# A sparse graph-attention kernel on one core: q copied a block ahead, list places read a step later, smaller last chunks, and the last block's values in one go

## The chip, the core and the metric

The kernel runs on one core of one Trainium2 chip. The time is the device time in microseconds (us) from the first to the last instruction; lower is better. The engines are named as in the profile: PE multiplies matrices, DVE does elementwise work and reductions, ACT does copies and nonlinear functions, POOL issues the indexed transfers (gathers), SP issues plain ones. Each engine works through its own list of instructions in the order in which the program emits them and waits on semaphores for the others.

## The reference, cut to what matters

The input is a table x of 3327 rows by 256 and an adjacency matrix of 3327 by 3327 in which about 0.5% of the entries are one. Layer 0 is a simple attention with one score per row; layers 1 to 3 are graph transformer layers of one form with weights of their own:

```python
# layers 1, 2, 3 (8 heads of 32)
qkv = layer_norm(x, g1, be1) @ w_qkv
q, k, v = ...
scores = einsum('nhd,mhd->hnm', q, k) * SCALE
scores = where(adj != 0, scores, -inf)
attn = softmax(scores, axis=-1)
out = einsum('hnm,mhd->nhd', attn, v).reshape(n, 256)
x = x + out @ w_proj + b_proj
h2 = layer_norm(x, g2, be2)
x = x + gelu(h2 @ w1 + b1) @ w2 + b2          # w1: 256 x 1024
```

## The kernel before

The kernel does not form the 3327 by 3327 scores. A first stage (layer 0 included) reads the adjacency matrix, makes for each row the list of its neighbours (up to 40), and sorts the rows by the length of their lists: `place` below is where a row's rank in that sort is read from counts that PE has summed up in PSUM. The sorted rows stand in 26 blocks of 128; a block needs as many slots as its longest list has entries, from 40 down to 10, 448 slots in all. Block 0, with 40 slots, comes last in the order of work.

In each of layers 1 to 3 the k and v rows of the neighbours are fetched slot by slot with indexed gathers on POOL (448 a layer), four slots to a tile, ten tiles in a ring (121 tiles a layer). A tile's way:

```python
def scores(self, b, s0):                     # one tile: k.q on DVE
    ...
    nc.vector.tensor_mul(k, k, self.q[b]...)                 # line 1320
    nc.vector.tensor_reduce(self.sc[b][:, s0:s0 + n, :], ...)  # line 1321
def softmax(self, b):                        # after a block's last tile
    nc.vector.tensor_tensor_reduce(sc, sc, pad[b]..., mx)    # line 1332
    nc.scalar.activation(sc, sc, AF.Exp, bias=mx, scale=-1.0)  # line 1335
def take_q(self, b):                         # q of a block into PSUM, two buffers
    nc.scalar.copy(self.q[b], t2[:, b, D:2 * D])             # line 1306
def weights(self, b):  ...                   # 1/sum on DVE, lines 1341 to 1348
def values(self, b, s0):                     # one tile: weighted v, summed on PE
    nc.vector.tensor_mul(vw, v, self.wp[b]...)               # line 1361, vw has 3 buffers
    for s in range(0, n, 2):
        nc.tensor.matmul(self.po[b], ident, vw[...])         # line 1366
    self.issue()                             # the tile is free: gathers of a later one
    if s0 + GS >= S:
        self.short += self.block(b)          # projection of the block, 9 short steps
```

`block(b)` queues nine short steps (copy, fold, transpose, copy, project on PE at line 1402, and at the end the add into x on DVE at line 1406). When the last block of a *chunk* has been added, the chunk's long steps are queued: layer norm, transposes, the two feed-forward products with gelu (lines 1445, 1451, 1468; PE works on all rows of the chunk at once), the add (line 1486), and, if a layer follows, its layer norm and q, k, v products (line 1498), after which k and v go to memory. `some()` is called once per tile and spreads these steps over the tiles of the blocks that follow; `rate` is how much of them is taken per tile:

```python
for n in [CB - 1] + [CB] * ((NB - CB - 2) // CB) + [2, 1]:   # 3, 4,4,4,4,4, 2, 1 blocks
    ...
# in add(), at the end of a chunk:
at = ORDER.index(b) + 1
turns = sum(len(slots[i]) for i in ORDER[at:at + CB])
turns = 5 if at == NB - 1 else turns - 2
self.rate = sum(cost for cost, _ in self.long) / max(turns, 1)

def some(self):
    if self.short: self.short.pop(0)()
    self.credit = min(self.credit + self.rate, 8.0)
    while self.long and self.credit > 0:
        cost, step = self.long.pop(0); self.credit -= cost; step()
    if self.short: self.short.pop(0)()

def run(self):
    ...
    for k, b in enumerate(ORDER):
        for g in slots[b]:
            self.scores(*g)
            if g == slots[b][-1]:
                self.softmax(b)
                if k + 1 < NB: self.take_q(ORDER[k + 1])
            for i in wait: wait[i] += 1
            for _ in range(2 if len(todo) > NBUF // 2 or b == 0 else 1):
                if todo and wait[todo[0][0]] > 1: value()
            self.some()
        todo += slots[b]; wait[b] = 0
    while todo:                              # the ten tiles of block 0
        value()
        self.some()
    self.rate = 4.0
    while self.short or self.long: self.some()
```

A layer's gathers read the k and v of all rows, so the next layer's first gather comes after the last chunk of the layer before.

Of the kernel before, what the change touches and what calls it, by code (L numbers as in the profile page):

```python
# [8 lines left out]
FP = mybir.dt.float32  # L9
# [3 lines left out]
ALU = mybir.AluOpType  # L13
AX = mybir.AxisListType
# [3 lines left out]
P = 128  # L18
# [14 lines left out]
NB = (N + P - 1) // P  # L33
# [25 lines left out]
NBUF = 10  # L59

CB = 4
# [462 lines left out]
def sparse_path(ctx, tc, ins, out, dram, flag):  # L524
    nc = tc.nc
# [13 lines left out]
    rank = const.tile([P, NB], FP, name="rank")  # L539
# [83 lines left out]
    with tc.tile_pool(name="a", bufs=1) as a, tc.tile_pool(name="aw", bufs=2) as aw, \  # L623
# [56 lines left out]
        nd = LMAX + 1  # L680
# [3 lines left out]
        OH = a.tile([P, NB, nd], BF, name="OH")  # L684
        rest_tri = a.tile([P, P], BF, name="rest_tri")
# [155 lines left out]
        class Group:  # L841
# [36 lines left out]
            def soft(self):  # L878


                g, n, b0 = self.g, self.n, self.blocks[0]

                def sv(name):
                    t = aw.tile([P, 4], FP, tag="s_" + name, bufs=1, name=f"s_{name}_{g}")
                    return t[:, :n]

                sg = S.s[:, b0:b0 + n]
                dg = deg[:, b0:b0 + n]
                nc.vector.tensor_copy(dg, self.acc[:, :n, H0])
                top = sv("top")  # L890
                nc.vector.tensor_scalar(top, dg, float(LMAX), None, ALU.min)
                nc.vector.tensor_tensor(OH[:, b0:b0 + n, :],
                                        num[:, None, :nd].to_broadcast([P, n, nd]),
                                        top[:, :, None].to_broadcast([P, n, nd]), ALU.is_equal)

                at = places[:, :4 * nd].rearrange("p (b k) -> p b k", k=nd)
                for j in range(n):
                    i = b0 + j
                    add = [(tri, i)] + [(ones_bf, k) for k in range(b0, i)]
                    if g:  # L900
                        add += [(rest_tri, i - 4)] + [(ones_bf, k) for k in range(i - 3, b0)]
                    for lhsT, m in add:
                        nc.tensor.matmul(at[:, j, :], lhsT, OH[:, m, :], start=False, stop=True,
                                         skip_group_check=True)
                t = aw.tile([P, 4, nd], FP, tag="place", bufs=1, name=f"place_{g}")[:, :n]
                nc.vector.tensor_mul(t, at[:, :n, :], OH[:, b0:b0 + n, :])
                nc.vector.tensor_reduce(rank[:, b0:b0 + n], t, AX.X, ALU.add)
                if b0 + n == NB:
                    nc.tensor.matmul(at[:, n - 1, :], rest_tri, OH[:, NB - 1, :], start=False,
                                     stop=True, skip_group_check=True)  # L910
                    S.all = at[:, n - 1, :]
                non, ga, fa, m1, m0, tt, mx = (
                    sv(k) for k in ("non", "ga", "fa", "m1", "m0", "tt", "mx"))
                nc.vector.tensor_scalar(non, dg, -1.0, float(N), ALU.mult, ALU.add)
                nc.vector.tensor_scalar(ga, dg, 0.0, None, ALU.is_gt)
                nc.vector.tensor_scalar(fa, non, 0.0, None, ALU.is_gt)
                nc.vector.tensor_scalar(tt, ga, -NEG0, NEG0, ALU.mult, ALU.add)
                nc.vector.tensor_mul(m1, sg, ga)
                nc.vector.tensor_add(m1, m1, tt)
                nc.vector.tensor_scalar(tt, fa, -1.0, 1.0, ALU.mult, ALU.add)  # L920
                nc.vector.tensor_mul(m0, sg, tt)
                nc.vector.scalar_tensor_tensor(m0, fa, NEG0, m0, ALU.mult, ALU.add)
                nc.vector.tensor_max(mx, m1, m0)
                nc.vector.tensor_sub(m1, m1, mx)
                nc.vector.tensor_sub(m0, m0, mx)
                nc.scalar.activation(m1, m1, AF.Exp)
                nc.scalar.activation(m0, m0, AF.Exp)
                self.non, self.m1, self.m0, self.tt = non, m1, m0, tt

            def mix(self):  # L930
# [12 lines left out]
                nc.vector.tensor_sub(t3, S.hsum[:, None, :].to_broadcast(shape), acc[:, :n, :H0])  # L943
                nc.vector.tensor_mul(t3, t3, m0[:, :, None].to_broadcast(shape))
                nc.vector.tensor_mul(nb, acc[:, :n, :H0], m1[:, :, None].to_broadcast(shape))
                nc.vector.tensor_add(nb, nb, t3)

            def project(self):
                g, n = self.g, self.n
# [312 lines left out]

    ORDER = [b for k in range(NB // 2) for b in (NB - 1 - k, k + 1)][:NB - 1] + [0]
    CHUNK, at = {}, 0
    for n in [CB - 1] + [CB] * ((NB - CB - 2) // CB) + [2, 1]:
        for b in ORDER[at:at + n]:
            CHUNK[b] = ORDER[at:at + n]
        at += n
# [3 lines left out]
    class Layer:  # L1272
# [101 lines left out]
        def block(self, b):  # L1374
            L, w, c = self.L, self.w, {}
            x = t2[:, b, :D]
            chunk = CHUNK[b]
            if b == chunk[0]:
                self.n2 = Norm(len(chunk), f"f{L}_{b}")
            n2 = self.n2  # L1380

            def copy():
                c["o"] = work.tile([P, D], FP, tag="o", name=f"o_{L}_{b}")
                nc.scalar.copy(c["o"], self.po[b][:, :D])

            def fold():
                nc.vector.tensor_add(c["o"], c["o"], self.po[b][:, D:])

            def turn():
                for k in range(2):  # L1390
                    nc.tensor.transpose(self.po[b][:, k * P:(k + 1) * P],
                                        c["o"][:, k * P:(k + 1) * P], ident)

            def copy_T():
                c["oT"] = work.tile([P, 2 * P], FP, tag="oT", name=f"oT_{L}_{b}")
                nc.scalar.copy(c["oT"], self.po[b][:, :2 * P])

            def project():
                ps = self.po[b][:, D:]
                nc.tensor.matmul(ps, ones_bf[:96, :], bias3[:, 0, :], start=True, stop=False)  # L1400
                for k in range(2):
                    nc.tensor.matmul(ps, c["oT"][:, k * P:(k + 1) * P], w["w_proj"][:, k, :],  # L1402
                                     start=False, stop=(k == 1))

            def add():
                nc.vector.tensor_add(x, x, self.po.pop(b)[:, D:])  # L1406
                n2.stats(chunk.index(b), x)
                if b == chunk[-1]:
                    self.long += self.chunk(chunk, n2)
                    at = ORDER.index(b) + 1  # L1410
                    turns = sum(len(slots[i]) for i in ORDER[at:at + CB])
                    turns = 5 if at == NB - 1 else turns - 2
                    self.rate = sum(cost for cost, _ in self.long) / max(turns, 1)

            return [lambda: None, copy, lambda: None, fold, turn, copy_T, project, lambda: None, add]
# [146 lines left out]
        def run(self):  # L1562
# [10 lines left out]

            for k, b in enumerate(ORDER):
                for g in slots[b]:
                    self.scores(*g)
                    if g == slots[b][-1]:
                        self.softmax(b)
                        if k + 1 < NB:
                            self.take_q(ORDER[k + 1])  # L1580
                    for i in wait:
                        wait[i] += 1
                    for _ in range(2 if len(todo) > NBUF // 2 or b == 0 else 1):
                        if todo and wait[todo[0][0]] > 1:
                            value()
                    self.some()
                todo += slots[b]
                wait[b] = 0
            while todo:
                value()  # L1590
                self.some()
            self.rate = 4.0
            while self.short or self.long:
                self.some()
# [45 lines left out]
```

## Time and profile before

| | us |
|---|---|
| median of 3 runs | 2787.56 (2777.72 to 2789.45) |
| profiled execution | 2779.3 |
| first stage with layer 0, to the first gathers of k and v | 0 to about 526 |
| layer 1: last tile scored / next layer's first gather | 1193.7 / 1303.5 |
| layer 2: first gather / last tile scored / next layer's first gather | 1303.5 / 1964.4 / 2074.6 |
| layer 3: first gather / last tile scored / end | 2074.6 / 2695.3 / 2779.3 |

PE is busy for 1952.0 us, DVE for 1961.9, POOL for 1361.8 and ACT for 806.5. No engine is near the whole span: which one ends the waiting changes from stage to stage. In the rows of busy tenths each digit stands for 69.5 us. In a timeline or group line, `kv<-kv,q` is out<-in, and the text in brackets is the idle time of the engine just before, with what ended it. A line number is that of the kernel before.

### The profile page before, as it was taken

Reading aid. Unit: us, or ns where it says so; the run is one execution under the profiler, and the core shown is the slowest. Engines: PE = TensorE matmul, PEld = TensorE weight load, DVE = VectorE, ACT = ScalarE, POOL = GpSimd, SP = SyncE. Lnnn points to the kernel's source line nnn. Section 1 sums busy time; section 2 is a strip of 40 time slices with the busy share of each in tenths; the row PEclk is TensorE's granted clock in tenths of the full one; section 3 lists DMA queues with packets and bytes.
Section 4 is the critical chain, followed back from the end, with each engine's and each line's share of the span. In section 5 each row is a group of like instructions: output and inputs, shape, how many; then the busy total and the mean of one; then the engine's idle time right before and its main releaser. Section 6 shows DMA issues by size and latency. Waiting matters only on the chain. (4 is left out here: it accounts for less than half of the span.)

```text
span 2779.3 us, 21889 instructions
## 1 busy us (share of the span) xinstructions
PE 1952.0 (70%) x6409; PEld 1045.3 (38%) x6409; DVE 1961.9 (71%) x4061; ACT 806.5 (29%) x1398; POOL 1361.8 (49%) x1458
## 2 busy tenths in 40 slices
PE   5657665248788887884377887887853678867866
PEld 4546553114333333442133443433431333333334
DVE  6597888577877777733788677778427878778852
ACT  5346552102332322321022332232320222222221
POOL 4000000377766666601776565566017777776741
PEclk9768776678899898897788898898976898988988
DMA  6224420677766666613776565566227766666650
GB/s 235 99 106 154 155 81 32 198 217 217 222 196 200 202 182 186 182 34 100 209 211 201 168 195 180 158 190 178 50 70 210 210 183 199 201 190 184 198 130 15
DMA packets 144478, 453.66 MB, mean 163 GB/s; under 512 B 29521, under 2 KB 40156, under 8 KB 141021
## 3 DMA queue, kind: packets, MB, share of 16 engines
q0 software_dynamic: 113056, 370.26, 46.0%
q1 hardware_dynamic: 9834, 53.90, 5.5%
q10 hardware_dynamic: 21458, 28.02, 2.9%
q8 instruction: 52, 0.85, 0.1%
q14 instruction: 78, 0.64, 0.1%
HBM read 420.64 MB, written 31.42 MB: 163 GB/s over the span
## 5 line engine op out<-in xcount | busy, mean ns | idle before, releaser
L1298 POOL DMA_INDIRECT kv<-kv,t x1344 | 1272.8, 947 | 810.0 <-issue 350.4
L1366 PE MATMUL po<-vw,s_ident 128*128 128x512 f32 (+1 forms) x1380 | 770.4, 694 | 497.4 <-DVE vw L1361 447.6
L1320 DVE TENSOR_TENSOR kv<-kv,q 128x1024 f32<-128x1024 f32 (+3 forms) x363 | 413.3, 1139 | 312.6 <-ACT q L1306 156.5
L1366 PEld LDWEIGHTS po<-vw,s_ident 128*128 128x128 f32 x1380 | 285.3, 220 | 846.5 <-issue 468.3
L1321 DVE TENSOR_REDUCE sc<-kv 128x32 f32<-128x1024 f32 (+3 forms) x363 | 414.1, 1141 | 12.4
L1361 DVE TENSOR_TENSOR vw<-kv,w 128x1024 f32<-128x1024 f32 x333 | 371.3, 1127 | 0.2
L1445 PE MATMUL pu<-fT,s_w 128*128 128x512 f32 (+3 forms) x768 | 308.1, 536 | 1.0 <-ACT fT L596 1.0
L1468 PE MATMUL py<-gT,s_w 128*128 128x512 f32 (+2 forms) x672 | 283.4, 549 | 0.0
L1451 ACT ACTIVATE gT<-pu,pvb 128x512 f32<-128x512 f32 (+3 forms) x192 | 116.4, 607 | 361.0 <-PE pu L1445 360.7
L1445 PEld LDWEIGHTS pu<-fT,s_w 128*128 128x128 f32 x768 | 150.6, 206 | 140.5 <-issue 116.0
L711 POOL MEMSET s_abf<- 128x1 bf16 x23 | 2.2, 105 | 375.2 <-DVE s_v L731 248.3
L1468 PEld LDWEIGHTS py<-gT,s_w 128*128 128x128 f32 x672 | 127.6, 191 | 122.0 <-issue 104.4
L723 PE MATMUL s_ptb<-s_ident_bf,s_abf 128*128 128x128 bf16 x676 | 69.8, 273 | 77.3 <-ACT s_abf L714 64.0
L735 DVE MAX8 cand<-s_v 128x8 f32<-128x208 bf16 x416 | 118.0, 359 | 0.9
L588 ACT ACTIVATE xn_f<-t,nm_f,rqy_f 128x256 f32<-128x256 f32 x78 | 42.9, 593 | 247.5 <-DVE nm_f L582 240.1
L1498 PE MATMUL pk<-s_w_qkv,nT 128*128 128x512 f32 x208 | 104.4, 626 | 8.9 <-ACT nT L596 8.9
L1335 ACT ACTIVATE sc<-sc,mx 128x120 f32<-128x120 f32 (+6 forms) x78 | 32.0, 410 | 259.8 <-DVE mx L1332 259.2
L1406 DVE TENSOR_TENSOR t<-t,po 128x256 f32<-128x256 f32 x78 | 32.5, 417 | 103.8 <-PE po L1402 97.9
L1486 DVE TENSOR_TENSOR t<-t,pd 128x256 f32<-128x256 f32 x75 | 29.5, 408 | 91.0 <-PE pd L1482 91.0
L723 PEld LDWEIGHTS <-s_abf 128*128 128x128 bf16 x676 | 58.8, 125 | 91.8 <-ACT s_abf L714 70.8
L855 PE MATMUL s_pa<-s_aT,s_hs 128*128 128x256 bf16 x338 | 80.4, 286 | 13.2 <-DVE s_hs L817 13.2
L724 ACT COPY s_aT<-s_ptb 128x896 bf16<-128x896 bf16 x104 | 82.7, 859 | 19.9 <-PE s_ptb L723 19.7
(292 smaller groups left out, 2343.5 us busy)
## 6 DMA issues: line engine op xcount, KB each, us to landing
s_a<-in_adj_dram SPq DMA_DIRECT2D x25, 1663.5 KB
kv<-kv,t POOLq DMA_INDIRECT x1344, 3.7
kv<-kvr ACTq DMA_DIRECT2D x52, 256.0 KB
kv<-s_kvr ACTq DMA_DIRECT2D x26, 256.0 KB
s_w<-in_L_gnn_w_dram SPq DMA_DIRECT2D x6, 1024.0 KB
t<-ql ACTq DMA_DIRECT2D x6, 592.0 KB
t<-s_x ACTq DMA_DIRECT2D x6, 512.0 KB
s_w_qkv<-in_L_gnn_w_qkv_dram SPq DMA_DIRECT2D x3, 768.0 KB
```

The lines of the kernel that those rows point to most:

```text
L723: nc.tensor.transpose(pt[:, m, :], self.abf[:, k * P:(k + 1) * P], ident_bf)
L724: nc.scalar.copy(aT[:, k0:k0 + len(ks), :], pt[:, :len(ks), :])
L735: nc.vector.max(out=self.cand[:, s, :], in_=self.v[:, s, :])
L1298: nc.gpsimd.indirect_dma_start(out=t[:, s, :], out_offset=None, in_=kv[L], in_offset=bass.IndirectOffsetOnAxis(ap=t2[:, b, k:k + 1].bitcas ...
L1320: nc.vector.tensor_mul(k, k, self.q[b][:, None, :].to_broadcast([P, n, D]))
L1321: nc.vector.tensor_reduce(self.sc[b][:, s0:s0 + n, :], k.rearrange("p s (h d) -> p s h d", d=HD), AX.X, ALU.add)
L1361: nc.vector.tensor_mul(vw[:, :n * D].rearrange("p (s h d) -> p s h d", h=HEADS, d=HD), v, self.wp[b][:, s0:s0 + n, :, None].to_broadcast([ ...
L1366: nc.tensor.matmul(self.po[b][:, :m], ident, vw[:, s * D:s * D + m], start=(s0 + s == 0), stop=(s0 + s + 2 >= S), skip_group_check=True)
L1445: nc.tensor.matmul(c["pu", f][:, :n], w["w1"][:, e, f * P:(f + 1) * P], c["hT"][:, e, :n], start=(e == 0), stop=(e == 1))
L1451: nc.scalar.activation(g[:, :n], c.pop(("pu", f))[:, :n], AF.Gelu_apprx_tanh, bias=w["b1"][:, f:f + 1])
L1468: nc.tensor.matmul(c["py"][e][:, :n], w["w2"][:, f, e * P:(e + 1) * P], g[:, :n], start=(f == 0), stop=last)
L1498: nc.tensor.matmul(ps[:, :c1 - c0], c["hT"][:, e, j * P:(j + 1) * P], nxt["w_qkv"][:, e, c0:c1], start=(e == 0), stop=(e == 1))
```

## The change

Four things are changed. (1) q of the next block is copied at the second tile of the block before it, instead of after its last tile and its softmax. (2) In the first stage, the reading of `place` moves from `soft` to the end of `mix`, which comes one half-step later. (3) The last chunks are 2, 2, 2, 1 blocks instead of 4, 2, 1, each spread over the tiles of the chunk that follows, whatever its size; in the last two blocks two tiles' values are done per tile scored, and the first of them need not wait for a second tile. (4) The ten value tiles of the last block are emitted one after the other, without long or short steps between them. The aim is that DVE waits less for ACT and PE, and that less is left to do between one layer's last tile and the next layer's first gather.

```diff
@@ Group.soft
-                t = aw.tile([P, 4, nd], FP, tag="place", bufs=1, name=f"place_{g}")[:, :n]
-                nc.vector.tensor_mul(t, at[:, :n, :], OH[:, b0:b0 + n, :])
-                nc.vector.tensor_reduce(rank[:, b0:b0 + n], t, AX.X, ALU.add)
-                if b0 + n == NB:
-                    nc.tensor.matmul(at[:, n - 1, :], rest_tri, OH[:, NB - 1, :], ...)
-                    S.all = at[:, n - 1, :]
+            def place(self):
+                ...                           # the same lines
@@ Group.mix
                 nc.vector.tensor_add(nb, nb, t3)
+                self.place()
@@ chunks
-    for n in [CB - 1] + [CB] * ((NB - CB - 2) // CB) + [2, 1]:
+    for n in [CB - 1] + [CB] * 4 + [2, 2, 2, 1]:
@@ block, add
-                    turns = sum(len(slots[i]) for i in ORDER[at:at + CB])
-                    turns = 5 if at == NB - 1 else turns - 2
+                    turns = sum(len(slots[i]) for i in CHUNK[ORDER[min(at, NB - 1)]]) - 2
@@ run
                 for g in slots[b]:
+                    if g == slots[b][1] and k + 1 < NB:
+                        self.take_q(ORDER[k + 1])
                     self.scores(*g)
                     if g == slots[b][-1]:
                         self.softmax(b)
-                        if k + 1 < NB:
-                            self.take_q(ORDER[k + 1])
                     for i in wait:
                         wait[i] += 1
-                    for _ in range(2 if len(todo) > NBUF // 2 or b == 0 else 1):
-                        if todo and wait[todo[0][0]] > 1:
+
+                    last = k >= NB - 2
+                    for _ in range(2 if len(todo) > NBUF // 2 or last else 1):
+                        if todo and wait[todo[0][0]] > (not last):
                             value()
                     self.some()
                 ...
             while todo:
                 value()
-                self.some()
```

More of the change, by code (lines that the diff above doesn't have):

```diff
@@ L904, in soft @@
                                          skip_group_check=True)
-                t = aw.tile([P, 4, nd], FP, tag="place", bufs=1, name=f"place_{g}")[:, :n]
-                nc.vector.tensor_mul(t, at[:, :n, :], OH[:, b0:b0 + n, :])
-                nc.vector.tensor_reduce(rank[:, b0:b0 + n], t, AX.X, ALU.add)
-                if b0 + n == NB:
-                    nc.tensor.matmul(at[:, n - 1, :], rest_tri, OH[:, NB - 1, :], start=False,
-                                     stop=True, skip_group_check=True)
-                    S.all = at[:, n - 1, :]
                 non, ga, fa, m1, m0, tt, mx = (
@@ L928, in soft @@
                 self.non, self.m1, self.m0, self.tt = non, m1, m0, tt
+            def place(self):
+                g, n, b0 = self.g, self.n, self.blocks[0]
+                at = places[:, :4 * nd].rearrange("p (b k) -> p b k", k=nd)
+                t = aw.tile([P, 4, nd], FP, tag="place", bufs=1, name=f"place_{g}")[:, :n]
+                nc.vector.tensor_mul(t, at[:, :n, :], OH[:, b0:b0 + n, :])
+                nc.vector.tensor_reduce(rank[:, b0:b0 + n], t, AX.X, ALU.add)
+                if b0 + n == NB:
+                    nc.tensor.matmul(at[:, n - 1, :], rest_tri, OH[:, NB - 1, :], start=False,
+                                     stop=True, skip_group_check=True)
+                    S.all = at[:, n - 1, :]
             def mix(self):
```

## The prediction

> **What bounds the kernel now.** I read the page's rows of busy tenths first, then the waits of DVE by stage, then the timelines of one steady stretch and of a layer's end.
>
> ```profile
> PE   5657665248788887884377887887853678867866
> DVE  6597888577877777733788677778427878778852
> POOL 4000000377766666601776565566017777776741
> ```
>
> POOL's row shows the layers: three stretches of gathers from slice 7 on, with two holes of zeros (slices 17 and 28) and a falling end. In the holes nothing is fetched; DVE falls to 3 and 2. Inside the stretches POOL stands at 5 to 7. When it issues without pause a gather takes 1.25 us (from 2074.57 to 2075.82 and on, 0.94 busy and 0.30 between), so 448 gathers take at least 560 us; layer 2 takes 660.9 from its first gather to its last tile scored, layer 3 620.7. So gathers limit only parts of the layers.
>
> The waits of the whole run (total, times, longest):
>
> ```profile
> DVE kv L1320 <- ACT q L1306: 156.5, 42, 7.3
> DVE kv L1320 <- DMA kv<-kv,t: 147.0, 67, 6.9
> DVE t L1406 <- PE po L1402: 97.9, 36, 6.6
> DVE place L906 <- PE places L903: 41.1, 7, 16.2
> ```
>
> The first wait and the last are what parts (1) and (2) aim at. By stage, the q waits are about 65 us in layer 1, 63 in layer 2 and 30 in layer 3, where gather waits are more common. What a q wait is worth depends on who is really behind. A stretch of layer 2, in windows of 50 us (PE, PEld, DVE, ACT, POOL busy; then clock, DMA share, GB/s):
>
> ```profile
> 1700.00:1750.00 50.00, 42.76 (x109) 19.43 (x108) 41.94 (x67) 15.86 (x27) 34.09 (x37) 0.93 0.63 193
> 1750.00:1800.00 50.00, 38.82 (x101) 18.47 (x100) 32.34 (x62) 13.66 (x23) 27.37 (x29) 0.83 0.56 165
> ```
>
> and the waits that lie in it, from the timeline:
>
> ```profile
> 1736.90 1.22 DVE L1320 TENSOR_TENSOR kv<-kv,q 128x1024 f32<-128x1024 f32 x1 [4.86 <-ACT q L1306]
> 1754.98 1.22 DVE L1320 TENSOR_TENSOR kv<-kv,q 128x1024 f32<-128x1024 f32 x1 [1.88 <-ACT q L1306]
> 1765.50 0.42 DVE L1406 TENSOR_TENSOR t<-t,po 128x256 f32<-128x256 f32 x1 [6.33 <-PE po L1402]
> 1779.95 3.78 PE L1366 MATMUL po<-vw,s_ident 128*128 128x512 f32 x4 [4.79 <-DVE vw L1361]
> 1795.75 1.22 DVE L1320 TENSOR_TENSOR kv<-kv,q 128x1024 f32<-128x1024 f32 x1 [6.17 <-ACT q L1306]
> 1811.05 1.99 PE L1366 MATMUL po<-vw,s_ident 128*128 128x512 f32 x4 [1.44 <-DVE vw L1361]
> ```
>
> A chunk of four repeats every 103 us or so. From 1724 to 1769 PE has no gap (the chunk's feed-forward): there PE sets the pace, DVE waits, and the first two q waits lie inside it. From 1770 to 1826 PE waits for DVE again and again, and the third q wait (6.17 us), at the chunk's q, k, v products, lies where DVE sets the pace.
>
> The end of layer 2:
>
> ```profile
> 1963.13 1.22 DVE L1321 TENSOR_REDUCE sc<-kv 128x32 f32<-128x1024 f32 x1
> 2000.98 1.23 DVE L1361 TENSOR_TENSOR vw<-kv,sc 128x1024 f32<-128x1024 f32 x1 [8.23 <-PE po L1366]
> 2021.56 0.42 DVE L1486 TENSOR_TENSOR t<-t,pd 128x256 f32<-128x256 f32 x1 [19.36 <-PE pd L1482]
> 2041.07 0.42 DVE L1387 TENSOR_TENSOR o<-o,po 128x256 f32<-128x256 f32 x1 [11.44 <-ACT o L1384]
> 2074.57 0.94 POOL L1298 DMA_INDIRECT kv<-kv,t  x1 [121.18 <-DVE s_row L1254]
> ```
>
> From the last tile scored (1964.35) to the next gather (2074.57) 110.2 us pass; layer 1's end has 109.8, layer 3's 84.0. The values of block 0 are strung out from 1968.5 to 2040.6, because long steps of two chunks stand between them in PE's list: the back half of the four-chunk (q, k, v from 1986.9 to 1999) and the whole two-chunk (feed-forward from 2002.9 to 2020.4). Only then comes block 0's own chain, 34 us (2040.67 to 2074.57).
>
> [...] the q copy at 1736.51 needs nothing but old data, yet it comes after an oT copy that had waited for PE (1734.50), a table load and the Exp. [...] here 101 loads for gelu and exp average 1283 ns, two of them around the q copy in the stretch above. [...]
>
> **Part 1, q.** The 78 copies (0.36 us each) stay; they move to where ACT has long slack. Removed waits only pay where DVE is behind. Waits at the q, k, v phase: layer 1 3.3, 6.2, 5.6, 6.1, 6.4; layer 2 3.8, 6.0, 6.1, 6.2, 6.4; together 56 us. I take 80%, 45 us, because PE runs without a gap for some 16 us after each and lets DVE run ahead only three vw buffers. The other 100 us: inside PE's feed-forward I count nothing, for the wait should turn up again at line 1406 (PE po L1402); in layer 3, with no q, k, v phase, nothing, since gathers are next. Sum: 45.
>
> **Part 2, places.** Seven waits, 41.1 us: 16.2 and 0.9 in the first 200 us, then 13.6, 4.1, 3.1, 2.6 and less. From 250 to 500 DVE is busy 41 to 47 us of each 50, and from 200 on it hardly waits for anything else, so the later 24 us are worth their whole; the read now comes after 13 small operations and a half-step of 5 to 7 us. Of the first wait I count a third, as ACT and PE are behind there too. Sum: 30.
>
> **Parts 3 and 4, the ends.** I followed the emission by hand with the costs in the code. Now, at the last tile the four-chunk stands at its shift step and the two-chunk hasn't begun. Changed, chunks (19, 20) and (21, 22) are wholly emitted before the last tile, and chunk (23, 24) has got to its second product; then ten values, then its rest. The path at layer 2's end, from the last tile: softmax and weights to the first PE value 4.5 us (now 5.6, with an add in it); ten values on PE at 1.72 (pace from the steady stretch) plus 2 for the slow start, 19: t = 23.5. The rest of the two-chunk's products, 15 at 0.86, and block 0's projection 2: 38.5. Shift, transposes, add, norm, q, k, v, as now from 2020.4 to 2037.6 without the 3.4 of a value group: 14, t = 52.5. Block 0's chunk from its xn (2047.32) to the gather: 27.3. Total 80 for 110: 30 saved, at two ends. Layer 3 has no q, k, v: 38.5 + 2, then 24.5 as now (2754.8 to 2779.3): 65 for 84, 19 saved.
>
> What it costs: the work has to go into the last 28 tiles. In layer 2 these took from 1820 to 1964 with DVE busy 108 of 144 us and PE 119. About 12 us of DVE (two norms of 2.6, adds and statistics) and 14 us of PE come in, one more chunk's fixed cost among them. Also the four-chunk before is now squeezed into 9 tiles instead of 18, a PE-bound run of 60 us or more where it was 46. Against it, gathers for the last tiles start a tile earlier. I charge 5 us a layer. Sum: 30 + 30 + 19 - 15 = 64.
>
> Together 45 + 30 + 64 = 139; 2787.56 - 139 = 2648.6, rounded to 2650.
>
> **Rivals.** (a) *The q waits are real everywhere.* Then all 156 us go, and with the rest the time is near 2540. For it: the wait is the largest one of DVE. Against it: PE is without a gap around two waits in three, and where POOL issues without pause DVE only waits for DMA sooner. (b) *Waits change names.* Line 1406, den waiting for Exp (now 0.0, but with `last` the weights follow Exp at once), and DMA take over; the squeezed four-chunk and the two-chunks lengthen the last 28 tiles by 15 to 20 us a layer and eat most of the 30. Then only places and some 30 us are left: 2720. For it: PE is busy 119 of 144 already. Against it: DVE waited 30 us in that stretch, so there is room. (c) *One go hurts.* Ten values in a row keep PE from the two-chunk's rest for 17 us; if chunk (23, 24) is what ends last, that delay is on the path. I have it in the sum; without it, a further 5 to 10 us could be had. It speaks against a large gain, not for a loss.
>
> **Range and chances.** The ends rest on durations from the trace and should hold to 8 us each; the q part may be 25 to 100, the places 15 to 40, the charge for the squeeze 0 to 20 a layer. That gives 2595 to 2715. A loss would need rival (b) at its worst and places worth nothing. Faster by over 2% means below 2731.8: 0.88; within 2%: 0.10; slower: 0.02.
>
> **What would show each step.** Right: `kv L1320 <- ACT q` near 0, but `t L1406 <- PE po` grown from 97.9 to 130 or more; the chunk cycle down from 103 to about 98 us; `place L906` below 12 us and the first gather about 30 us sooner, near 496; the three ends 80, 80 and 65 us; layer 2's gathers-to-last-tile 640 or so. Wrong: an end above 95; L1406 unchanged while layers shrink by 50 us (rival a); a layer's stretch not shorter although q waits are gone, with DMA or den waits in their place (rival b).

## The result and the profile after

The changed kernel takes 2856.21 us (median of 4 runs, 2853.08 to 2862.57), the kernel before beside it 2785.89: a ratio of 1.026, 95% interval 1.023 to 1.0289. The change makes the kernel slower. The forecast of 2650 us missed in size and in sign.

The first reading is where the time went. Each layer is cut in two: the *stream*, from its first gather to its last tile scored, and the *end*, from there to the next layer's first gather (or the end of the run). Profiled executions, us:

| | before | after | difference |
|---|---|---|---|
| up to the first gather | 525.0 | 504.0 | -21.0 |
| streams of layers 1, 2, 3 | 668.6, 660.9, 620.7 | 743.3, 738.7, 644.3 | +74.7, +77.8, +23.6 |
| ends of layers 1, 2, 3 | 109.8, 110.2, 84.1 | 80.0, 80.5, 70.0 | -29.8, -29.7, -14.1 |
| span | 2779.3 | 2860.8 | +81.5 |

The start and the ends gave 95 us together, of the 109 foreseen for them. The streams lost 176 us. The busy tenths of the changed kernel, a slice now being 71.5 us:

```profile
PE   5757774257977877773478778777672678877866
DVE  6698997587776774653777776656636878778563
POOL 4000000776755753603775465455307777777560
```

The holes on POOL between the layers are at slices 17 and 29 now. Ahead of each of them POOL falls to 3 (slices 15 and 28), and in layer 2 it stands at 4 and 5 from slice 24 on, where it had 5 and 6: the second half of a layer crawls. DVE falls to 4 to 6 in these slices, and PE has 6 to 8: neither is full. The work has hardly grown either:

```profile
PE 1985.0 (69%) x6601; PEld 1083.7 (38%) x6601; DVE 1972.3 (69%) x4126; ACT 828.4 (29%) x1444; POOL 1362.5 (48%) x1458
```

DVE is busy 10 us longer than before and PE 33 us, in a span that is 81 us longer. So most of what was lost is waiting. The waits of DVE in the changed kernel (total, times, longest):

```profile
DVE t L1411 <- PE po L1407: 215.8, 45, 12.9
DVE kv L1325 <- DMA kv<-kv,t: 127.7, 71, 7.3
DVE kv L1325 <- ACT q L1311: 113.8, 26, 8.5
DVE t L1411 <- ACT q L1311: 36.6, 6, 6.4
DVE den L1346 <- ACT sc L1340: 24.4, 5, 5.9
DVE place L927 <- PE places L903: 6.5, 2, 3.9
```

Lines 1325 and 1411 are lines 1320 and 1406 of before. The place wait is down from 41.1 to 6.5. The wait for q has not gone: 113.8 us stay, although q is copied a block ahead. The add's wait for the projection has more than doubled (97.9 before), and the wait of `den` for Exp is new. ACT's own list has the other side of the q wait:

```profile
ACT q L1311 <- DVE kv L1325: 64.0, 30, 13.8
```

The q copy now waits for DVE, and DVE for the q copy. In a stretch of layer 2, from the timeline:

```profile
1573.90 0.69 ACT L1455 ACTIVATE gT<-pu,pvb 128x512 f32<-128x512 f32 x1 [4.21 <-PE pu L1449]
1574.49 0.38 ACT L1311 COPY q<-t 128x256 f32<-128x256 f32 x1
1574.89 1.22 DVE L1325 TENSOR_TENSOR kv<-kv,q 128x1024 f32<-128x1024 f32 x1 [3.32 <-ACT q L1311]
```

The product at 1574.89 is the second tile of a block whose q was copied a block earlier. What it waits for is the copy of the *next* block's q, which it does not read, and that copy stands on ACT behind a gelu that has waited 4.21 us for PE. In the code both q buffers are halves of one PSUM tile: `q2 = ps_q.tile([P, 2, D], FP)`, 2 KB per partition. In the trace none of the 78 q copies (376 to 389 ns each) overlaps in time with any of the 363 products that read q. That this comes of the shared tile is so far a guess; the run `q_banks` below tries it. The expectations call such a tile a bank, after the program's helper `bank`, which makes PSUM tiles of this size; where a tile lies in PSUM no trace shows.

### The profile page after: what moved, and what is told of

Same layout as the page of the kernel before. It is cut to its first block, busy times and chain, and to the rows that moved or that the text cites. A ratio compares the mean times of both kernels' runs of the same rounds, so it can differ in the third digit from the quotient of the medians.

```text
span 2860.8 us, 22448 instructions
## 1 busy us (share of the span) xinstructions
PE 1985.0 (69%) x6601; PEld 1083.7 (38%) x6601; DVE 1972.3 (69%) x4126; ACT 828.4 (29%) x1444; POOL 1362.5 (48%) x1458
## 5 line engine op out<-in xcount | busy, mean ns | idle before, releaser
L1371 PE MATMUL po<-vw,s_ident 128*128 128x512 f32 (+1 forms) x1380 | 784.1, 707 | 505.8 <-DVE vw L1366 443.6
L1455 ACT ACTIVATE gT<-pu,pvb 128x512 f32<-128x512 f32 (+3 forms) x216 | 122.9, 569 | 432.4 <-PE pu L1449 431.8
L1449 PEld LDWEIGHTS pu<-fT,s_w 128*128 128x128 f32 x864 | 165.5, 200 | 127.5 <-issue 94.6
L1411 DVE TENSOR_TENSOR t<-t,po 128x256 f32<-128x256 f32 x78 | 32.6, 418 | 254.2 <-PE po L1407 215.8
L1472 PEld LDWEIGHTS py<-gT,s_w 128*128 128x128 f32 x768 | 146.4, 192 | 110.5 <-issue 88.7
L1502 PE MATMUL pk<-s_w_qkv,nT 128*128 128x512 f32 x208 | 112.9, 669 | 7.6 <-ACT nT L596 7.6
L855 PE MATMUL s_pa<-s_aT,s_hs 128*128 128x256 bf16 x338 | 81.2, 288 | 13.2 <-DVE s_hs L817 13.2
L588 ACT ACTIVATE xn_n<-t,nm_n,rqy_n 128x256 f32<-128x256 f32 x52 | 28.6, 593 | 201.2 <-DVE nm_n L582 184.7
L1407 PE MATMUL po<-s_w_proj,oT 128*128 128x256 f32 x312 | 86.0, 400 | 0.0
```

Of the source, the lines that this page charges most:

```text
L1371: nc.tensor.matmul(self.po[b][:, :m], ident, vw[:, s * D:s * D + m], start=(s0 + s == 0), stop=(s0 + s + 2 >= S), skip_group_check=True)
L1449: nc.tensor.matmul(c["pu", f][:, :n], w["w1"][:, e, f * P:(f + 1) * P], c["hT"][:, e, :n], start=(e == 0), stop=(e == 1))
L1455: nc.scalar.activation(g[:, :n], c.pop(("pu", f))[:, :n], AF.Gelu_apprx_tanh, bias=w["b1"][:, f:f + 1])
L1472: nc.tensor.matmul(c["py"][e][:, :n], w["w2"][:, f, e * P:(e + 1) * P], g[:, :n], start=(f == 0), stop=last)
L1502: nc.tensor.matmul(ps[:, :c1 - c0], c["hT"][:, e, j * P:(j + 1) * P], nxt["w_qkv"][:, e, c0:c1], start=(e == 0), stop=(e == 1))
```

## The experiments

Theory A: the early q copy costs time because both q buffers share a PSUM tile, so that DVE, ACT and PE wait for each other in a ring. Theory B (the prediction's rival b): the smaller last chunks lengthen the last tiles of a layer by more than the ends give back; the expectations from `chunks_back_b` on call this theory C. A third view, tried by `places_q` and `places_q2`: q's waits are worth what the prediction said, and something else took the gain. Below, *the rule* is the change for the last two blocks in part (3) (two tiles' values per tile scored, and sooner), rival L of the expectations, and *the one go* is part (4). All kernels here are edits of before or of after. The runs from `chunks_back_b` to `places_q` and from `spread4_last` to `spread4_oldq_b` fell to times in which the kernel before itself takes 3270 to 3297 us at a granted clock of 0.785 (2780 us and 0.836 otherwise; the expectations put this down to a slower chip, which the record does not show: chip 5 gave 2781 us in one set and 3297 in another), so they are compared only as ratios or within their set.

**q alone.** Before, with q copied at the second tile of the block ahead; nothing else.

```diff
+                    if g == slots[b][1] and k + 1 < NB:
+                        self.take_q(ORDER[k + 1])
                     self.scores(*g)
                     if g == slots[b][-1]:
                         self.softmax(b)
-                        if k + 1 < NB:
-                            self.take_q(ORDER[k + 1])
```

> The kernel before with part 1 alone (q copied at the second tile of the block ahead). Theory A (the early copy itself costs: both q buffers are halves of one PSUM tile, so the program makes DVE's second tile of a block wait for ACT's copy of the next block's q, which in turn waits for DVE's first tile): q waits of DVE stay near 100 us instead of going to 0, they stand at second tiles, and the time rises by 30 to 80 us, to 2815 to 2865. Theory B (the chunks are what costs, the early copy is neutral or a small gain): 2740 to 2790, q waits near 0 in this kernel.

Measured: 2847.17 us, ratio 1.0244 (1.022 to 1.0267), 69 us above before beside it (2778.46). The streams are 703.5, 692.3, 621.3, the ends 111.0, 111.0, 87.7, near those of before. So part 1 by itself loses nearly all that the whole change loses. Its waits:

```profile
DVE t L1406 <- PE po L1402: 180.1, 41, 7.9
DVE kv L1320 <- ACT q L1306: 91.7, 26, 5.7
DVE t L1406 <- ACT q L1306: 47.8, 8, 6.4
```

Before, these three were 97.9, 156.5 and 5.8: 260 us. Now they are 320.

**q in two PSUM tiles.** The changed kernel, with q of one parity and the softmax weights w of the other parity sharing a tile, instead of both q in one and both w in the other.

```diff
-    q2 = ps_q.tile([P, 2, D], FP, name="q2")
-    w2 = ps_q.tile([P, 2, D], FP, name="w2")
+    qw = [ps_q.tile([P, 2, D], FP, name=f"qw{k}") for k in range(2)]
-            self.q[b] = q2[:, ORDER.index(b) % 2, :]
+            self.q[b] = qw[ORDER.index(b) % 2][:, 0, :]
-                wp = w2[:, ORDER.index(b) % 2, :S * HEADS]
+                wp = qw[(ORDER.index(b) + 1) % 2][:, 1, :S * HEADS]
```

> The changed kernel with the two q buffers in two PSUM banks (each bank holds q of one parity and the softmax weights of the other, which only DVE touches), so that copying the next q and reading this q no longer share a bank. Theory A: the waits of DVE for ACT q fall to under 10 us, those of ACT q for DVE kv too, the chunk cycle goes back to 103 us or below, and the time falls by 50 to 110 us, to 2745 to 2805. Theory B: the time stays within 20 us of 2856, since the waits turn up again at line 1411 behind PE.

Measured: 2777.56 us, 0.9994 (0.9979 to 1.0009): 79 us less than the changed kernel, all of it in the streams (698.6, 701.2, 640.9; ends 80.1, 80.6, 69.9). The products' wait for the q copy falls from 113.8 to 1.2 us, and 20 of the 78 copies now overlap in time with a product that reads the other q. A copy now waits for the value products that read the weights in its own PSUM tile (81.8 us of ACT's time), but DVE waits only 6.5 us there for a copy in return, so no ring closes. Theory A holds. What the copies and the products wait for is set by the PSUM tile that they share: by how it is declared, or by where it lies in PSUM, which the edit does not tell apart. With this mended the change is worth nothing: the streams are still 20 to 40 us a layer longer than before.

**Places alone**, on before, with the diff of part 2.

```diff
                 nc.vector.tensor_add(nb, nb, t3)
+                self.place()          # moved here from soft()
```

> The kernel before with part 2 alone. Both theories: the first gather of k and v comes some 24 us earlier (that is what the changed kernel shows), the layers are as before, so 2755 to 2770. If the layers lengthen by the same amount, 2786.

Measured: 2755.65 us, 0.9911 (0.9886 to 0.9935): 23 us saved, the first gather at 504.6 instead of 525.0. The wait is down from 41.1 to 5.3 us.

**q back.** The changed kernel with q at its old place, in one PSUM tile.

```diff
-                    if g == slots[b][1] and k + 1 < NB:
-                        self.take_q(ORDER[k + 1])
                         self.softmax(b)
+                        if k + 1 < NB:
+                            self.take_q(ORDER[k + 1])
```

> The changed kernel with q copied at the old place. Theory A: the chunk cycle is 103 us again and the last 28 tiles of a layer shorten too, 2740 to 2800. Theory B (the squeezed four-chunk and the two-chunks cost the whole): 2820 to 2860, with the last 28 tiles still near 190 us.

Measured: 2788.21 us, 1.003 (1.0011 to 1.005). With places, chunks, the rule and the one go, and without the q move, the kernel is no faster than before. The ends are 80.0, 80.7, 69.9, but the streams 712.3, 704.4, 640.8. So theory B is needed too. Against `q_banks`, q early and in two PSUM tiles is worth 11 us here.

**Chunks back, last rule back, V back, and before with places and q in two PSUM tiles.** The first three are `q_banks` with one part undone; the fourth is before with places and q early in two PSUM tiles, so without the chunks, the rule and the one go.

```diff
# chunks_back_b                                   # last_back
-[CB - 1] + [CB] * 4 + [2, 2, 2, 1]               -last = k >= NB - 2
+[CB - 1] + [CB] * ((NB - CB - 2) // CB) + [2, 1] +for _ in range(2 if ... or b == 0 else 1):
+turns = 5 if at == NB - 1 else turns - 2         +    if todo and wait[todo[0][0]] > 1:
# v_back
             while todo:
                 value()
+                self.some()
```

> The changed kernel with q in two banks (as in q_banks, 2777.6 us, streams 699, 701, 641 us from first gather to last tile scored, ends 80, 81, 70) and with the chunks and their pace as before (4, 2, 1; four-chunk over four blocks); places, values in one go and the rule for the last two blocks stay changed. Theory C (the small chunks and the squeezed four-chunk lengthen the stream, more than the end gives back): streams fall to 650 to 670, 645 to 665, 610 to 625, ends rise to 100 to 115 and 75 to 90, time 2730 to 2765. Rival L (the two-tiles rule of the last two blocks is what lengthens the stream): streams stay within 10 us of 699, 701, 641, and with longer ends the time is 2830 or more.

> q_banks with the old rule for how many values per tile and when, in the last two blocks; chunks 2, 2, 2, 1 and one go stay. Theory C: streams within 8 us of 699, 701, 641; the two-chunk begins a tile later, so ends 83 to 88; time 2775 to 2800. Rival L (each of two early den readings waits some 5.7 us for Exp, and more): streams 10 to 25 us shorter, time 2725 to 2765.

> q_banks with long and short steps between the ten values of the last block again. Streams unchanged (within 3 us) for both theories. If one go pays, as the prediction's sum has it, ends rise to 85 to 100 us and the time to 2790 to 2830. If it doesn't matter because the rest of chunk (23, 24) ends last anyway, ends stay at 78 to 82 and the time within 8 us of 2777.6.

> The kernel before with places read later and q copied early into two banks, chunks, pace, rule and values all as before. From places_alone (2755.7; streams 664, 664, 621; ends 110, 109, 88): if removing the q waits pays as predicted (part 1: 45 us, at the q, k, v products of layers 1 and 2 only), streams 641, 641, 621 and 2710. If the waits only move to line 1411 behind PE: streams within 6 us of 664, 664, 621 and 2745 to 2760. Theory C expects 2725 to 2750: q_back and q_banks differ by 14, 3 and 0 us of stream.

Measured, ratio to before in the same set: `chunks_back_b` 0.9777 (0.972 to 0.9834), `last_back` 0.9982 (0.9965 to 1.0), `v_back` 0.9962 (0.9944 to 0.998), `places_q` 0.9874 (0.9824 to 0.9925). Only with the old chunks does the time fall clearly. Streams of layers 1 and 2: 843.7 and 811.7 with the old chunks, 871.0 and 844.2 in `last_back`, 869.4 and 835.6 in `v_back`. So the chunks, not the rule or the one go, are what has to be undone. `q_banks` itself was not run in this set, so what the rule and the one go are worth does not come out of it.

**The same two again, and the packing by itself.** `chunks_back_b2` and `places_q2` are `chunks_back_b` and `places_q`. `squeeze_alone` is `places_q2`, old chunks and all, but with the fourth four-chunk's steps packed into the tiles of two blocks instead of four, as the change does (it is the fifth chunk in order, and the last four-chunk where the chunks are 2, 2, 2, 1; the expectations say "fifth four-chunk"):

```diff
                     turns = 5 if at == NB - 1 else turns - 2
+                    if at == NB - CB - 3:
+                        turns = sum(len(slots[i]) for i in ORDER[at:at + 2]) - 2
```

`spread4` is the other side: `q_banks`, with the chunks of 2, 2, 2, but that chunk's steps spread over four blocks again:

```diff
-                    turns = sum(len(slots[i]) for i in CHUNK[ORDER[min(at, NB - 1)]]) - 2
+                    turns = (sum(len(slots[i]) for i in ORDER[at:at + CB]) - 2 if len(chunk) > 2
+                             else sum(len(slots[i]) for i in CHUNK[ORDER[min(at, NB - 1)]]) - 2)
```

> The same kernel as chunks_back_b, on another chip if one is given: there before took 3275 us on a chip that showed 0.78 of the clock and long waits between engines, so its times can't be set beside the others. Theory C (small chunks lengthen the stream more than the end gives back): on a chip where before takes 2778, streams 650 to 665, 645 to 665, 610 to 625, ends 100 to 106 and 72 to 80, time 2715 to 2745, ratio 0.975 to 0.988. Rival L (the two-tiles rule): streams near 690, 690, 640 and 2830 or more.

> The same kernel as places_q, on another chip if one is given. From places_alone (ratio 0.991; streams 664, 664, 621): if the q waits are worth what the prediction counted (45 us), ratio 0.975 and streams 641, 641, 621. If they only move behind PE, 0.988 to 0.993. On the slower chip the ratio was 0.987, so I expect 0.984 to 0.989 and streams 650 to 658, 650 to 660, 618 to 622.

> places_q with chunks 4, 2, 1 as before, only the pace of the fifth four-chunk changed: its steps are packed into the tiles of the next two blocks (9 turns) and not four. If packing the four-chunk is what lengthens the stream in the changed kernel (44 us of stream in q_back against before), streams of layers 1 and 2 grow by 15 to 30 us over places_q2, with ends unchanged (109, 109, 87). If it is the work of two more two-chunks in front of the last tile (and the stalls of their own chains), they grow by less than 6 us.

> q_banks (streams 699, 701, 641; ends 80, 81, 70) with the fifth four-chunk spread over four blocks again, so that its second half and two-chunks (19, 20) and (21, 22) crowd the last 18 tiles. If packing the four-chunk costs, the streams fall by 10 to 25 us. If the two-chunks' work before the last tile costs, they stay within 8 us of 699, 701, 641 or grow. Ends 80, 81, 70 either way.

Measured, beside before at 2781.07:

| | us | ratio (95% interval) | streams | ends |
|---|---|---|---|---|
| chunks_back_b2 | 2735.85 | 0.9837 (0.9821 to 0.9853) | 663.6, 662.6, 620.9 | 104.5, 102.2, 73.8 |
| places_q2 | 2753.49 | 0.9899 (0.9883 to 0.9916) | 663.1, 659.5, 621.0 | 108.9, 108.7, 87.2 |
| squeeze_alone | 2781.14 | 1.0005 (0.9995 to 1.0016) | 667.7, 665.8, 635.0 | 110.7, 111.3, 84.6 |
| spread4 | 2736.73 | 0.984 (0.9816 to 0.9864) | 685.2, 688.0, 626.4 | 79.8, 80.1, 68.2 |

Four things follow. First, `places_q2` is not told from `places_alone` (0.9911): with the old chunks, taking q's waits away is worth about nothing. The waits of `places_q2` say where they went:

```profile
DVE t L1410 <- PE po L1406: 174.8, 41, 8.6
DVE t L1410 <- ACT qw L1310: 66.4, 8, 8.6
```

The add (line 1406 of before) now waits 241 us; in `places_alone` q and add together were 256. The second line is the same wait for PE, put down to a copy that ended at nearly the same moment: the add reads nothing of `qw`, and in all eight cases the projection ended 0.11 us before the add began, as it does in the 41 of the first line. One wait was taken away and the next one in DVE's list, for the same late engine, took its place. At one chunk's q, k, v products, where the prediction counted its gain, first in `places_alone`, then in `places_q2`:

```profile
1770.81 1.22 DVE L1325 TENSOR_TENSOR kv<-kv,q 128x1024 f32<-128x1024 f32 x1 [6.68 <-ACT q L1311]
1774.80 0.42 DVE L1411 TENSOR_TENSOR t<-t,po 128x256 f32<-128x256 f32 x1 [1.51 <-PE po L1407]
```

```profile
1766.56 0.42 DVE L1410 TENSOR_TENSOR t<-t,po 128x256 f32<-128x256 f32 x1 [8.36 <-PE po L1406]
```

The two waits, 8.2 us together, have become one of 8.4. Second, the one go and the rule, with the old chunks, shorten the ends by 4.4, 6.5 and 13.4 us and cost the streams 3 us at most: `chunks_back_b2` is the best version, with `spread4` equal to it. Third, the chunks lengthen the streams by 35.0, 38.6 and 20.0 us (`q_banks` less `chunks_back_b2`, which differ in the chunks and their pace alone); with the rule and the one go it is 35.5, 41.7 and 19.9 (`q_banks` less `places_q2`). Fourth, the packed four-chunk is 13.4, 13.2 and 14.5 us of that (`q_banks` less `spread4`); by itself, on old chunks, it costs 4.6, 6.3 and 14.0.

Where the 41.7 us of layer 2 lie is seen in one window each: from the start of the fourth four-chunk's layer norm to the last tile scored, first `places_q2`, then `q_banks` (PE, PEld, DVE, ACT, POOL busy; clock, DMA share, GB/s).

```profile
1788.74:1934.62 145.88, 124.79 (x314) 58.62 (x315) 103.51 (x170) 43.49 (x71) 84.13 (x89) 0.89 0.64 170
```

```profile
1797.34:1985.03 187.69, 145.94 (x430) 81.65 (x430) 115.12 (x224) 58.33 (x103) 84.20 (x89) 0.85 0.51 138
```

The same 26 tiles take 41.8 us longer. PE is busy for 21.1 us more in them and DVE for 11.6; but PE also idles for 41.8 us instead of 21.1, at a lower clock. About 2.4 of the 21.1 are the same 78 value products taking longer (44.8 us, then 47.2). So nearly half is work that came in, and half is new waiting. How it arises is in the timeline of `q_banks`, the last two blocks of layer 2 (waits of DVE and PE above 5 us, in order of time):

```profile
1895.75 0.40 DVE L1345 TENSOR_REDUCE den<-sc 128x8 f32<-128x136 f32 x1 [7.53 <-ACT sc L1339]
1914.46 5.73 PE L1370 MATMUL po<-vw,s_ident 128*128 128x512 f32 x8 [8.68 <-DVE vw L1365]
1929.78 0.38 DVE L1345 TENSOR_REDUCE den<-sc 128x8 f32<-128x128 f32 x1 [6.10 <-ACT sc L1339]
1960.76 0.42 DVE L1489 TENSOR_TENSOR t<-t,pd 128x256 f32<-128x256 f32 x1 [12.39 <-PE pd L1485]
1969.59 1.18 PE L591 MATMUL pn<-s_ident,xn_n 128*128 128x128 f32 x4 [8.87 <-ACT xn_n L588]
```

DVE and PE wait in turn. The Exp behind the first of these waits is ready early and starts late, as ACT's list shows:

```profile
1891.54 0.48 ACT L1454 ACTIVATE gT<-pu,pvb 128x256 f32<-128x256 f32 x1 [3.25 <-PE pu L1448]
1894.02 1.28 ACT L1339 ACT_TABLE_LOAD   x1
1895.31 0.41 ACT L1339 ACTIVATE sc<-sc,mx 128x136 f32<-128x136 f32 x1
```

Its input was there at 1884.70; it stands behind five gelus of the first two-chunk, each of which waits for PE (0.39 to 3.25 us), a copy and a table load of 1.28 us, and so starts 10.6 us later: ACT did not take it ahead of them. With the new rule DVE needs that Exp at once.

**What is left of the chunks' cost.** Three variants of `spread4`: `spread4_last` with the old rule for the last two blocks, `spread4_v` with steps between the last values, `spread4_oldq` with q at its old place in one PSUM tile (the diffs of `last_back`, `v_back` and `q_back`).

> spread4 with the old rule for values in the last two blocks (two values a group only for block 0, a value only after two groups), so that its stream has the 2, 2, 2 chunks but not the weights that follow Exp at once. If the rule is part of what still lengthens the streams by 22, 28 and 5 us over the old chunks, the streams come down by 5 us or more a layer, `den <- ACT sc` in the last two blocks of a layer is gone, the ends grow by less than that, and the time falls to 2725 or below. If the chunks' own work is all of it, the streams stay at 685, 688 and 626 within 3 us, the ends grow by 3 to 5 us and the time is 2740 to 2750.

> spread4 with the steps of the chunks put between the last values again. If the one go is worth what it was worth with the old chunks (4, 6 and 13 us), the ends grow by that and the time is about 2755. If with the 2, 2, 2 chunks little is left to stand between the values, the ends grow by 3 to 5 us each at most and the time is 2740 to 2748. The streams should stay.

> spread4 with q copied at its old place and kept in one bank, as before: the q waits are back. If these waits are worth nothing because PE's products set the pace (as places_q2 against places_alone, 2 us, says), the time stays within 8 us of spread4: 2732 to 2745. If the two-block chunks make DVE the one that is behind in the last stretch, the q waits count there and the time is 2755 or more.

They gave 0.9852 (0.9822 to 0.9881), 0.9934 (0.9907 to 0.996) and 0.996 (0.9939 to 0.998), without `spread4` beside them. So two of them were run again next to it:

> The same kernel as spread4, beside its own variants on one chip, since the last three runs fell to a chip on which everything takes 18% longer. On the chip of the first runs: about 2737 us, streams near 685, 688, 626 and ends near 80, 80, 68. On the slower chip: about 0.984 of before.

> The old rule for values in the last two blocks. Theory one, the rule adds nothing to the streams: streams as in spread4_b within 3 us, ends 3 to 5 us longer, time 5 to 12 us above spread4_b. Theory two, the rule is part of the 22, 28 and 5 us: streams 5 us or more a layer shorter, time below spread4_b. The run on the slower chip (0.9852, against 0.984 of spread4 on the other chip) leaves both open.

> q at its old place and in one bank. If q's place is worth nothing behind PE's products: within 8 us of spread4_b. If, as the slower chip's ratio (0.996 against 0.984) would have it, the waits for q do count once chunks are spread: 25 to 35 us above spread4_b, with the q waits of DVE back at 100 us or more in all and the streams 8 to 12 us a layer longer.

Measured, beside before at 3269.4: `spread4_b` 3242.83 us, 0.9918 (0.9901 to 0.9936), streams 872.1, 848.7, 784.8; `spread4_last_b` 3229.95 us, 0.9888 (0.9864 to 0.9911), streams 860.6, 833.7, 781.7, ends 85.2, 84.4, 70.0 (80.5, 79.9, 69.3 in `spread4_b`); `spread4_oldq_b` 3261.16 us, 0.9969 (0.9954 to 0.9984). The streams without the rule are 11.5, 15.0 and 3.1 us shorter, the ends 5 longer, and the wait of `den` for Exp is gone; in time the two intervals overlap a little. In layers 1 and 2 the rule takes more than it gives here. And q's waits (in `spread4_oldq_b` DVE waits 195.4 us for q) do count once there are chunks of two: 18 us, between the 8 or less of one theory and the 25 to 35 of the other. In time `spread4_v` does not stand out from `spread4_b`, but its ends are 86.4, 86.4, 71.8, which is 2.5 to 6.5 us longer. Over all sets the old chunks are the safer choice: `spread4` saves 1.6% in one set and 0.8% in the other, `chunks_back_b2` and `chunks_back_b` 1.6% and 2.2%.

## Why the prediction was wrong

These are the steps of its sum, with what the runs gave for each, in profiled us. The streams' part is split by `places_q2` less before, after less `q_banks`, and `q_banks` less `places_q2`:

| step | predicted | measured |
|---|---|---|
| places | -30 | -21.0 (first gather 525.0 to 504.0) |
| q waits | -45 | -6.6 by itself, +85.6 by the shared PSUM tile |
| ends | -30, -30, -19 | -29.8, -29.7, -14.1 |
| charge for the squeeze (chunks, rule, one go) | +15 | +97.1 (35.5, 41.7, 19.9) |
| sum | -139 | +81.5 |

**Places** were right in mechanism, and a little too large; the sign given for them, a wait below 12 us, came out (6.5), the first gather 504 rather than 496.

**The ends** were right to 5 us, and so was the path in them. In layer 2 the ten values come after the second product of chunk (23, 24) and ahead of the rest of them, as the hand-made emission said:

```profile
2066.05 0.49 DVE L1337 CUSTOM_DVE_ANT_1 sc<-sc,pads 128x320 f32<-128x320 f32 x1
2074.72 17.33 PE L1371 MATMUL po<-vw,s_ident 128*128 128x512 f32 x40
2091.89 1.03 PE L1449 MATMUL pu<-fT,s_w 128*128 128x256 f32 x4
2103.72 0.42 DVE L1411 TENSOR_TENSOR t<-t,po 128x256 f32<-128x256 f32 x1 [9.57 <-PE po L1407]
2146.53 0.94 POOL L1303 DMA_INDIRECT kv<-kv,t  x1 [112.20 <-DVE s_row L1259]
```

The values are done 25.9 us after the last tile (predicted 23.5; the 2 us in it for a slow start of PE did not come: the 40 products start 0.43 us apart from the first to the last, at a granted clock of 1.00), block 0's projection at 37.6 (38.5), and the gather comes at 80.5 (80). It comes 5.67 us after the write of block 0's k and v is issued (2140.86), as in the kernel before (2068.90 to 2074.57), so that write is most likely what it waits for, and the `s_row` in its brackets only ended at the same time. Only in layer 3 was the time without q, k, v taken 5 us too short. Rival (c) is not supported: with steps put between the values again (`spread4_v` against `spread4_b`) the ends were 2.5 to 6.5 us longer, not shorter.

**The q waits** are the first failed step: "Removed waits only pay where DVE is behind ... I take 80%, 45 us". It rests on the waits at the q, k, v phase being DVE's own. With the waits truly gone (`places_q2`), the streams gain 6.6 us, and the add's wait grows by as much as q's fell. At the q, k, v products, too, the projection that DVE needs next comes from PE at its own pace. PE waited for DVE in between (the 6.17 us wait at 1795.75 in the prediction lies among such waits), but that did not make DVE the bound of the stretch. The sign that the prediction itself named, line 1406 growing to 130 or more, is there (215.8), and the reading that belongs to it was rival (b). The sign named for being wrong, a stretch not shorter although the q waits are gone, came out in `places_q2`: 659.5 us in layer 2 for 660.9.

**A ring was not seen at all,** and this is the step that turned the gain into a loss. The prediction had "The 78 copies (0.36 us each) stay; they move to where ACT has long slack." It looked at when ACT is free, and not at what else uses the PSUM tile of the q buffers. Moved to the second tile, each copy lands between two products on DVE that read the other half of it. That is worth 79 us of time (after less `q_banks`). The chunk cycle, predicted to fall from 103 to 98, rose to 107 to 110 in layers 1 and 2; with two PSUM tiles it is 100 to 103 there.

**The charge of 5 us a layer** is the third failed step, and its size is what was wrong. The text had the right terms: 12 us of DVE (11.6 measured) and 14 of PE (21.1) come in, and "DVE waited 30 us in that stretch, so there is room". (Its figures for the stretch are a little off: in the trace of before it holds 26 tiles, not 28, DVE is busy for 104.0 us, not 108, and PE for 123.0, not 119.) There was room by the sums, but none by the order: these are chains, Exp to `den` to values to products to add to norm, of one chunk of two after another, and the timeline of `q_banks` above shows each engine waiting at its turn. That the order and not another cause makes the new waits is read from that timeline; no run tries it by itself. Rival (b) named this and gave it 15 to 20 us a layer; it was 35, 42 and 20. Of the whole, 41.1 us are the four-chunk packed into two blocks; of the other 56.0 the rule for the last blocks has a part, 29.6 us of stream in the set of `spread4_last_b`. How much it is beside `q_banks` was not measured. The range, too, was narrower than its own terms: all of them at their worst give 2753, not 2715.

## What to carry to other kernels

Two halves of one PSUM tile did not serve as two buffers here: none of the 78 copies ran beside a product that read the other half, and with q in two PSUM tiles the products' wait for the copy fell from 113.8 to 1.2 us. So look at what shares a PSUM tile before moving a write next to a read, and look for a pair of waits that point at each other (ACT q on DVE kv, DVE kv on ACT q). A wait that was taken away gave next to nothing where the next wait in the same engine's list ended at the same moment, so judge it by the sum of the neighbours (260 us before, 241 with q's waits gone). And work moved into a stretch where each of two engines idles is not free because there is idle time: it has to be checked as a chain, and the ends that it shortens set against the stream that it lengthens (74 us against 97 here).

## What the runs showed of the hardware

The same 1380 value products took longer in the kernels in which PE idled longer ahead of them. The group of value products in before, in the changed kernel and in `spread4` (busy, mean ns, idle time before and what ended it):

```profile
L1366 PE MATMUL po<-vw,s_ident 128*128 128x512 f32 (+1 forms) x1380 | 770.4, 694 | 497.4 <-DVE vw L1361 447.6 <-DVE rqv_f L551 49.3
```

```profile
L1371 PE MATMUL po<-vw,s_ident 128*128 128x512 f32 (+1 forms) x1380 | 784.1, 707 | 505.8 <-DVE vw L1366 443.6 <-DVE rqv_f L551 61.9
```

```profile
L1370 PE MATMUL po<-vw,s_ident 128*128 128x512 f32 (+1 forms) x1380 | 745.4, 677 | 424.2 <-DVE vw L1365 371.6 <-DVE rqv_f L551 51.9
```

The mean goes with the idle time ahead of them: 677 ns at 424 us, 694 at 497, 707 at 506; the granted clock of these runs is 0.838, 0.836 and 0.823. `q_alone` with 713 ns, 536 us and 0.822 lies on the same line: the products are busy for 795.8 us in it and for 770.4 in before, 25 us more for the same work. In `q_banks`, with the ring gone, the products take 689 ns after 451 us of idle time, at a clock of 0.832. Only `squeeze_alone`, with 701 ns after 515 us at 0.834, lies a little off.

The clock's record in before holds only the values 1.00 and 0.50. The 1054 value products that lie wholly in stretches at 1.00 take 587 ns on average, the 256 wholly at 0.50 take 1094; in the changed kernel 1006 take 587 and 282 take 1093. In before the clock is at 1.00 from 1727 to 1770 us, where PE is busy for 41.4 of 43 us, and four value products take 1.88 us at 1753.73; it is at 0.50 from 1778 to 1791, where PE is busy for 8.3 of 13 us between its waits, and four take 3.78 at 1779.95. Between 520 and 2700 us it falls to 0.50 68 times. In the 7 us ahead of these falls PE was busy for 50% on average, against 88% in the 7 us ahead of points at the full clock. So more idle time, a lower clock and longer products came together, and the idle time came first. Whether it is the cause was not shown: no run sets the clock by itself.
